# Eight steps instead of four in one tile of the bias product, and another order of the loads at the start

## The chip, the cores and the metric

The kernel runs on one core of a Trainium2 chip. The metric is the device time of one execution in microseconds (us). Five engines work side by side, each through its own list of instructions in order: TensorE (PE, matrix products), VectorE (DVE), ScalarE (ACT), GpSimd (POOL) and SyncE (SP). SP, ACT and POOL also issue DMAs, which 16 DMA engines carry out. An instruction that waits holds up all that stand behind it on its engine.

## What is computed

Four layers are computed one after the other on an image of 2 x 512 x 32 x 32. The change lies in the first, an attention with sampled keys. Cut to what matters:

```python
q    = gconv1x1(bn(x), qw)                     # 8 groups of 64 channels
off  = tanh(pw(gelu(dwconv(q)))) * 4           # where to sample: 8 x 8 points per image and group
kv   = grid_sample(bn(x), off)
k, v = gconv1x1(kv, kw), gconv1x1(kv, vw)
pos  = grid_q[:, :, None, :] - grid_kv[:, None, :, :]      # 1024 queries x 64 points, 2 numbers
bias = sign(pos) * log1p(abs(pos))
bias = relu(bias @ cpb_w1 + cpb_b1)            # 2 -> 128
bias = relu(bias @ cpb_w2 + cpb_b2)            # 128 -> 128
bias = bias @ cpb_w3 + cpb_b3                  # 128 -> 1
attn = softmax(q @ k.T * scale + bias)
x    = x + out_w @ (attn @ v) + out_b
...                                            # an MLP, then three more attention layers
```

The small network from 2 numbers to 1 runs for each of 16 (image, group) x 1024 x 64 pairs, and most of the first layer's time goes there.

## The kernel before

`layer0` holds the first layer. It begins with a top: loads, small products that prepare weights, and the folds of a later layer's weights (`fold`, `small_fold`, `transposed`). Then comes the long loop, `for i in range(steps)`, of 8 x 32 steps: 8 tile pairs t (two groups of one image), 32 steps for each, four points in each step.

A step has four parts, in the order 1, 0, 3, 2 (turns k = 0 to 3). For each, `second` (matmul at L621) multiplies the four points' first hidden layer, tiles `h1`, by 32 columns of `cpb_w2` into a PSUM tile z, and ScalarE (L630) writes its ReLU into a tile `h2`. `first` (L604, VectorE) makes `h1` some steps ahead in a ring of six tiles. `joined` (L635, VectorE) adds part 1 to part 0 and part 3 to part 2, with signs sorted beforehand so that a sum will do for the last weights. A DMA that accumulates, issued by GpSimd (L939, the join), adds the second sum to the first, in `joins[i]`.

`joins[i]` has 128 rows, 32 for each of four points, and all rows of one point are only to be summed with signs. So further DMAs fold it: L932 adds odd rows to even rows (64 rows are left), and four steps share one tile `whole`. The first step of four is folded once more in place (L934, 32 rows); of the others SP copies 32 rows into the tile (L936) and GpSimd adds the other 32 (L942). Then `third` (L650) multiplies four such tiles by `w3_16` into the PSUM tile sim, 16 steps in a call, two calls for each tile pair; `scores` (L658) adds q times k. GpSimd issues in a step the fold of step i-2 (turn 0), the join of i-1 (turn 1), the accumulation of i-3 (turn 1) and, in every fourth step, the second fold (turn 3). Each waits for the semaphore of the DMA whose data it reads. The last 16 steps (from `LAST`) share a tile by two.

`h2` of part 0, where the joins live, comes from two cycles, `h2j` (two slices of the tile `bridge` and two tiles of their own) and `h2p` (six slices of `bridge`); that of part 2, which the join reads, from the pool `h2b` with three tiles. z, and many small PSUM tiles, share a pool of three (`ps_z`, helper `zt`).

Other work of the layer is put between the parts, one piece after every second part, by `behind`, a chain of generators: `finish(t)` (softmax, projection at L710), `offsets(t + 2)` and `samples(t + 1)`. The order on each engine is that of the program text; no planner moves it.

In the top, SP loads the small weights: `load_groups("qw")` and `("kw")` fill the diagonal blocks of tiles that GpSimd has set to zero before, and they are the third to sixth DMA of SP. ScalarE loads x's first quarter and the fold weights. Query weights scaled by the normalisation (`qws`) are kept for all four pairs, and value weights (`vwbd`) too.

Of the kernel before, what the change touches and what calls it, by code (L numbers as in the profile page):

```python
# [19 lines left out]
P = 128  # L20
# [59 lines left out]
def kernel(ctx: ExitStack, tc: tile.TileContext, a: dict, out: bass.AP):  # L80
# [111 lines left out]
    def layer0(l0, fold_d, t2_b, o2_b):  # L192
# [7 lines left out]
        h2p = cycle([bridge[:, k, :] for k in range(6)])  # L200
        h2j = cycle([bridge[:, 6, :], bridge[:, 7, :], *(one.tile([P, HW], F32, name=f"h2j{k}") for k in range(2))])
# [16 lines left out]
        nc.scalar.dma_start(out=xs[0][:, 0, :], in_=a["x"][0, 0:P, :])  # L218
        qkv2, proj2 = load_w(wa, "wa", [a["qkv2_w"], a["proj2_w"]], nc.scalar)
        qkw = next(h2j).rearrange("p (j q n) -> p j q n", j=2, q=NPAIR)  # L220
        vw = one.tile([P, NPAIR, P], F32, name="vwbd")
        bd = {"qw": qkw[:, 0], "kw": qkw[:, 1], "vw": vw}
        for w in bd.values():
            nc.gpsimd.memset(w, 0.0)

        def load_groups(name):
            for h in range(2):
                r = slice(h * DH, (h + 1) * DH)
                nc.sync.dma_start(out=bd[name][r, :, r], in_=a[name][:, r, :].rearrange("q p o -> p q o"))

        load_groups("qw")
        load_groups("kw")
# [4 lines left out]
        ring += [qkv2.rearrange("p k n -> p (k n)")[:, k * 2 * HW : (k + 1) * 2 * HW] for k in range(3)]  # L237
        ring.append(proj2.rearrange("p k n -> p (k n)"))
        vb2 = one.tile([P, CC], F32, name="vb2")
        with nc.allow_non_contiguous_dma("512 numbers"):  # L240
            nc.sync.dma_start(out=vb2, in_=a["vb"][1].rearrange("(k p) -> p k", p=P))
        nc.sync.dma_start(out=xs[0][:, 1:, :], in_=a["x"][0, P:, :].rearrange("(k p) n -> p k n", p=P))

        def late_loads():
            load_groups("vw")
            nc.sync.dma_start(out=xs[1], in_=a["x"][1].rearrange("(k p) n -> p k n", p=P))
# [7 lines left out]
        qws = one.tile([P, NPAIR, P], F32, name="qws")  # L254
        nc.vector.tensor_scalar(qws[:, 0, :], bd["qw"][:, 0, :], s1[:, 0:1], None, ALU.mult)
        qb = one.tile([P, NPAIR], F32, name="qb")
        pqb = zt([P, NPAIR], "pqb")
        for pr in range(NPAIR):
            nc.tensor.matmul(pqb[:, pr : pr + 1], bd["qw"][:, pr, :], col("bn1_b", pr), start=True, stop=True)
        nc.vector.tensor_copy(qb, pqb)  # L260
# [16 lines left out]
        w3_16 = one.tile([P, 48], F32, name="w3_16")  # L277
# [7 lines left out]
        def bias_weights():  # L285
# [5 lines left out]
            few = one.tile([P, 28], F32, name="few")  # L291
# [69 lines left out]
            quarter = few[:, 26:28]  # L361
            for k in range(2):
                nc.vector.tensor_reduce(quarter[:, k : k + 1], ident[:, 2 + k : P : 4], AX.X, ALU.add)
                nc.vector.scalar_tensor_tensor(eighth, quarter[:, k : k + 1], 8.0, eighth, ALU.mult, ALU.add)
            nc.vector.tensor_scalar(w3_16[:, 16:32], row[:, 0:16], eighth, 0.0, ALU.add, ALU.is_equal)
            nc.vector.tensor_scalar(w3_16[:, 16:32], w3_16[:, 16:32], w3sign[:, 1:2], None, ALU.mult)
# [15 lines left out]
        def offsets(t):  # L382
# [4 lines left out]
            for half in range(2):  # L387
                n = slice(half * HALF, (half + 1) * HALF)
                nc.tensor.matmul(pq[:, n], qws[:, pr, :], xs[b][:, pr, n], start=True, stop=True)
# [60 lines left out]
            pos = two.tile([P, 2, 32], F32, name="pos")  # L450
# [14 lines left out]
            sgn = two.tile([P, 2, 32], F32, name="sgn")  # L465
# [19 lines left out]
        def samples(t):  # L485
# [5 lines left out]

            gp = gps.pop(t)
# [7 lines left out]
            near = two.tile([P, 2, 32], F32, name="near")  # L500
            wsum = two.tile([P, 3], F32, name="wsum")
            for ax in range(2):
                nc.scalar.activation(near[:, ax, :], ir, AF.Abs, bias=gp[:, ax : ax + 1], scale=-1.0)
                nc.scalar.activation(
                    near[:, ax, :], near[:, ax, :], AF.Relu, bias=1.0, scale=-1.0, accum_out=wsum[:, ax : ax + 1]
                )
            nc.vector.tensor_mul(wsum[:, 2:3], wsum[:, 0:1], wsum[:, 1:2])
# [33 lines left out]
            nc.tensor.matmul(pkv[:, 1, :], bd["vw"][:, pr, :], kv, start=True, stop=True)  # L541
# [17 lines left out]
        NCH = NR // 4  # L559
        LAST = NT * NR - 16  # L560
        tabs_of = {}

        def load_tabs(c):
# [4 lines left out]
            for ax in range(2):  # L568
                src = slog_d[t, ax].rearrange("(q r) i -> q r i", q=4)
                tab = (one if ax else two).tile([P, 16, 32], F32, name=f"tab{ax}")  # L570
                if 4 * c < LAST:
                    q, r = rc % 4, rc // 4 * 16
# [41 lines left out]
        def second(i, h1s, part):  # L614
# [13 lines left out]
            ring = h2q if part % 2 else h2b if part else h2j if i % (4 if i < LAST else 2) else h2p  # L628
            h2 = ring.tile([P, HW], F32, name="h2", tag="h2") if ring in (h2q, h2b) else next(ring)
# [10 lines left out]
        def third(sim, r, h2s, fours=(), halves=range(2), wide=False):  # L640

            for half in halves:
                n = slice(half * HALF, (half + 1) * HALF)
                w = w3_16[:, 16 - r : 48 - r] if wide else w3[:, 24 - r : 56 - r]
# [17 lines left out]
        def finish(t, sim):  # L662

            b, pr = divmod(t, NPAIR)
            if pr == 0:
                aTs[b] = one.tile([P, NPAIR, HW], F32, name="aT")
            simb = one.tile([P, HW], F32, name="simb", tag="wy")
# [22 lines left out]
            nc.vector.tensor_tensor(atv, atv, sm.unsqueeze(2).to_broadcast([P, 16, NJ]), ALU.mult)  # L690
            yield
# [85 lines left out]
        def transposed(j, k):  # L777
# [4 lines left out]
            for i in range(2):  # L782
                nc.scalar.copy(nat[j][i][:, :, k * P : (k + 1) * P], tw[:, 2 * i : 2 * i + 2, :])
# [4 lines left out]
        def key_weights():  # L788
# [15 lines left out]

        steps = offsets(0)
        advance(steps, 2)
        bias_steps = bias_weights()
        next(bias_steps)
        key_steps = key_weights()
        advance(key_steps)  # L810
        advance(steps, 4)
        advance(bias_steps)
        advance(steps, 20)
        drain(key_steps)
        nc.vector.tensor_tensor(
            qws[:, 1:], bd["qw"][:, 1:], s1[:, 1:].unsqueeze(2).to_broadcast([P, NPAIR - 1, P]), ALU.mult
        )
# [3 lines left out]
        nat = [[next(h2p).rearrange("p (k n) -> p k n", k=2) for _ in range(2)] for _ in range(3)]  # L821
        wq, wk, wv = [lambda o, n, w=w: w[o // 2][:, o % 2, n] for w in nat]
        everything = slice(0, C)
        pb2 = ps_s.tile([P, CC], F32, name="pb2", tag="sim")
# [19 lines left out]
        def small_fold():  # L844

            row = zt([P, C], "row")
            for o in range(CC):
                nc.tensor.matmul(
                    row[:, o * P : (o + 1) * P], col("qkv2_b", o).to_broadcast([P, P]), ident, start=True, stop=True
                )  # L850
            yield
# [4 lines left out]
            for m in range(CC):  # L856
                n = slice(m * P, (m + 1) * P)
                accumulate(pb2[:, m : m + 1], [(proj2[:, o, n], vb2[:, o : o + 1]) for o in range(CC)])
                yield
            nc.vector.tensor_tensor(o2_b, pb2, col("proj2_b", 0, CC), ALU.add)  # L860

        fold_steps, small_steps = fold(), small_fold()
        for k in range(CC):
            for j in range(3):
                transposed(j, k)

        advance(fold_steps)
        drain(bias_steps)
        advance(steps)
        advance(fold_steps)  # L870
        drain(steps)
        advance(small_steps)
        advance(fold_steps)
        advance(small_steps)
# [3 lines left out]
        for _ in range(5):  # L878
            advance(fold_steps)
            advance(small_steps)  # L880
        drain(fold_steps)

        steps = NT * NR
        h1s, parts, joins, sim, w1s = {}, {}, {}, None, None  # L890
        behind = chain(small_steps, offsets(1), samples(0))
# [5 lines left out]
        for i in range(steps):  # L897
            for k, part in enumerate((1, 0, 3, 2)):
# [5 lines left out]
                due = i - 20  # L904
                if k == 1 and 0 <= due < LAST and due % 16 == 0:
                    t, r = divmod(due, NR)
                    if r == 0:
                        sim = ps_s.tile([P, HW], F32, name="sim")
                    third(sim, r, [joins.pop(due + j) for j in range(0, 16, 4)], wide=True)
                    if r:  # L910
# [10 lines left out]
                if LAST <= i - 2 and i < steps - 2:  # L921
# [4 lines left out]
                    if i - 3 >= LAST and i % 2 and k == 3:  # L926
                        nc.gpsimd.dma_start(out=joins[i - 3][1:P:2], in_=joins.pop(i - 2)[1:P:2], accum_op=ALU.add)
                if 0 <= i - 2 < LAST:
                    j = (i - 2) % 4
                    whole, own = joins[i - 2 - j], joins[i - 2]  # L930
                    if k == 0:
                        nc.gpsimd.dma_start(out=own[0:P:2], in_=own[1:P:2], accum_op=ALU.add)  # L932
                    if k == 3 and j == 0:
                        nc.gpsimd.dma_start(out=own[0:P:4], in_=own[2:P:4], accum_op=ALU.add)  # L934
                    if k == 3 and j:
                        nc.sync.dma_start(out=whole[j:P:4], in_=own[0:P:4])  # L936
# [3 lines left out]
                j = (i - 3) % 4  # L940
                if k == 1 and 0 <= i - 3 < LAST and j:
                    nc.gpsimd.dma_start(  # L942
                        out=joins[i - 3 - j][j:P:4], in_=joins.pop(i - 3)[2:P:4], accum_op=ALU.add
                    )
# [5 lines left out]
                if k == 1 and due == LAST:  # L950
                    third(sim, 16, [joins.pop(due + j) for j in range(0, 8, 2)])
# [1325 lines left out]
```

## Time and profile before

| | |
|---|---|
| time, median of 3 runs | 3342.97 us (3342.06 to 3345.39) |
| the profiled execution: its time, its span | 3343.91 us, 3342.0 us |
| matmuls of L621 (z) | 16384, 593 ns each; four run side by side |
| chain that ended last: TensorE's share, L621's share | 96%, 52% |
| the loop | from 57.4 to about 1968 us |
| DMA engines' busy share, 400 to 1000 us | 0.79 |
| software queue (GpSimd's DMAs), whole span | 68400 packets, 231.26 MB |

A line of the page reads: line of the code, engine, operation, output<-input, count, busy time and mean length, then how long the engine stood idle just before such instructions and what ended that. In a timeline a line begins with start and length. The length of a DMA instruction is that of its issue; when its data has landed is seen from what waits for it.

### The profile page before, as it was taken

Reading aid. Unit: us, or ns where it says so; the run is one execution under the profiler, and the core shown is the slowest. Engines: PE = TensorE matmul, PEld = TensorE weight load, DVE = VectorE, ACT = ScalarE, POOL = GpSimd, SP = SyncE. Lnnn points to the kernel's source line nnn. Section 1 sums busy time; section 2 is a strip of 40 time slices with the busy share of each in tenths; the row PEclk is TensorE's granted clock in tenths of the full one; section 3 lists DMA queues with packets and bytes.
Section 4 is the critical chain, followed back from the end, with each engine's and each line's share of the span. In section 5 each row is a group of like instructions: output and inputs, shape, how many; then the busy total and the mean of one; then the engine's idle time right before and its main releaser. Section 6 shows DMA issues by size and latency. Waiting matters only on the chain.

```text
span 3342.0 us, 60958 instructions
## 1 busy us (share of the span) xinstructions
PE 3319.8 (99%) x24813; PEld 1605.2 (48%) x24813; DVE 2640.9 (79%) x3029; ACT 1809.4 (54%) x2774; POOL 675.3 (20%) x803
## 2 busy tenths in 40 slices
PE   9999999999999999999999999999999999999999
PEld 4333333333333333333333339999953443687777
DVE  6999999999998799999999966455446465765556
ACT  4866877877876677877867642112126245122221
POOL 1333333333333233333333210000000000000000
PEclk9999999999999999999999999999999999999999
DMA  5777877787787577778877741000100000000111
GB/s 171 158 162 161 162 164 156 158 169 152 160 166 158 107 165 151 161 165 160 166 159 152 161 120 58 14 9 12 51 0 14 26 32 17 7 7 4 29 33 36
DMA packets 142482, 343.91 MB, mean 103 GB/s; under 512 B 36465, under 2 KB 51441, under 8 KB 141425
## 3 DMA queue, kind: packets, MB, share of 16 engines
q0 software_dynamic: 68400, 231.26, 37.1%
q1 hardware_dynamic: 72496, 103.95, 10.1%
q8 instruction: 197, 3.23, 0.4%
q10 hardware_dynamic: 1296, 4.72, 0.4%
q14 instruction: 93, 0.75, 0.1%
HBM read 71.46 MB, written 10.83 MB: 25 GB/s over the span
## 4 chain that ended last, share of the span: by engine, by line
PE 96%; DVE 1%; issue 1%; ACT 1%; DMA 1%; SPq 0%; POOL 0%; DVEq 0%; ACTq 0%; POOLq 0%
PE z L621 52%; PE pma L135 6%; PE pw L1440 6%; PE pmb L135 5%; PE pmv L1440 4%; PE score L1619 3%; PE pv L1631 3%; PE pm L1440 3%; PE score L1440 3%; PE ppr L1440 1%; PE pmt L1440 1%; PE sim L650 1%; PE pf L135 1%; PE pp L710 1%; PE pma L1343 1%
## 5 line engine op out<-in xcount | busy, mean ns | idle before, releaser
L621 PE MATMUL z<-wa,cpb_w 128*32 128x512 f32 x10880 | 1191.9, 593 | 2.7 <-ACT h L630 2.7
L630 ACT ACTIVATE h<-z,b2h 128x1024 f32<-128x1024 f32 x768 | 851.1, 1113 | 331.0 <-PE z L621 301.7
L604 DVE CUSTOM_DVE_ANT_1 wa<-tab,pairs 128x2048 f32<-128x2048 f32 x340 | 776.4, 2284 | 3.1 <-PE z L621 2.6
L621 PEld LDWEIGHTS z<-wa,cpb_w 128*32 128x32 f32 x10880 | 346.5, 110 | 809.3 <-issue 712.4
L621 PE MATMUL z<-h,cpb_w 128*32 128x512 f32 x5504 | 609.5, 593 | 0.7 <-ACT h L630 0.7
L604 DVE CUSTOM_DVE_ANT_1 h<-tab,pairs 128x2048 f32<-128x2048 f32 x172 | 392.7, 2284 | 1.7 <-PE z L621 1.5
L621 PEld LDWEIGHTS z<-h,cpb_w 128*32 128x32 f32 x5504 | 175.1, 110 | 407.9 <-issue 362.7
L635 DVE SCALAR_TENSOR_TENSOR h<-h,turn,h 128x1024 f32<-128x1024 f32 x256 | 327.1, 1278 | 5.5 <-ACT h L630 5.5
L630 ACT ACTIVATE bridge<-z,b2h 128x1024 f32<-128x1024 f32 x162 | 180.8, 1116 | 119.0 <-PE z L621 119.0
L932 POOL DMA_DIRECT2D bridge<-bridge x150 | 127.5, 850 | 539.5 <-DMA bridge<-h 517.5
L635 DVE SCALAR_TENSOR_TENSOR bridge<-bridge,turn,h 128x1024 f32<-128x1024 f32 x162 | 207.0, 1278 | 4.3 <-ACT bridge L630 4.3
L939 POOL DMA_DIRECT2D bridge<-h x161 | 158.4, 984 | 247.0 <-DVE h L635 151.8
L1283 ACT COPY p<-pma 128x128 f32<-128x128 f32 x80 | 21.3, 266 | 334.7 <-PE pma L135 334.7
L1275 DVE TENSOR_TENSOR upper<-pma,p 128x256 f32<-128x256 f32 x80 | 33.7, 421 | 178.6 <-ACT p L1283 178.5
L1620 ACT ACTIVATE p<-score 128x512 f32<-128x512 f32 x256 | 130.0, 624 | 81.2 <-PE score L1619 79.4
L932 POOL DMA_DIRECT2D h2j<-h2j x90 | 76.2, 846 | 314.7 <-DMA h2j<-h 292.6
L630 ACT ACTIVATE h2j<-z,b2h 128x1024 f32<-128x1024 f32 x94 | 104.9, 1116 | 41.5 <-PE z L621 41.5
L1652 DVE TENSOR_TENSOR acc<-acc,p 128x1024 f32<-128x1024 f32 x96 | 111.0, 1217 | 19.5 <-ACT p L1620 19.2
L1619 PE MATMUL score<-q,k 64*128 64x512 f32 x512 | 120.7, 604 | 1.1 <-DVE gm L1196 1.1
L635 DVE SCALAR_TENSOR_TENSOR h2j<-h2j,turn,h 128x1024 f32<-128x1024 f32 x94 | 120.1, 1278 | 0.0
L1631 PE MATMUL pv<-p,vT 128*64 128x512 f32 x512 | 116.5, 598 | 0.0
L942 POOL DMA_DIRECT2D bridge<-bridge x90 | 111.1, 1235 | 0.2 <-issue 0.2
(460 smaller groups left out, 4379.4 us busy)
## 6 DMA issues: line engine op xcount, KB each, us to landing
bridge<-h POOLq DMA_DIRECT2D x161, 512.0 KB, 5.5
h2j<-h POOLq DMA_DIRECT2D x94, 512.0 KB, 5.5
bridge<-bridge POOLq DMA_DIRECT2D x159, 256.0 KB, 3.7
tab<-slog_d SPq DMA_DIRECT2D x128, 256.0 KB, 5.0
h2j<-h2j POOLq DMA_DIRECT2D x90, 256.0 KB, 3.3
bridge<-bridge POOLq DMA_DIRECT2D x150, 128.0 KB, 5.4
bridge<-bridge SPq DMA_DIRECT2D x90, 128.0 KB, 3.6
bridge<-h2j SPq DMA_DIRECT2D x90, 128.0 KB, 3.7
```

What stands on the lines that cost most here:

```text
L135: nc.tensor.matmul(pm, w, m, start=(k == 0), stop=(k == len(pairs) - 1))
L604: nc.vector._custom_dve(TENSOR_ADD_SAT, out=h1, in0=tx.unsqueeze(1).to_broadcast([P, H, 2, W]), in1=ty.unsqueeze(3).to_broadcast([P, H, 2, ...
L621: nc.tensor.matmul(z[point * 32 : point * 32 + 32, n], cpb_w2[:, lo : lo + 32], h1s[point][:, half * 16 : half * 16 + 16, :], start=True, ...
L630: nc.scalar.activation(h2, z, AF.Relu, bias=b2h[:, part : part + 1])
L635: nc.vector.scalar_tensor_tensor(h2, h2, turn[:, part // 2 : part // 2 + 1], parts.pop(part + 1), ALU.mult, ALU.add)
L932: nc.gpsimd.dma_start(out=own[0:P:2], in_=own[1:P:2], accum_op=ALU.add)
L939: nc.gpsimd.dma_start(out=joins[i - 1], in_=other, accum_op=ALU.add)
L942: nc.gpsimd.dma_start(out=joins[i - 3 - j][j:P:4], in_=joins.pop(i - 3)[2:P:4], accum_op=ALU.add)
L1440: nc.tensor.matmul(out, stationary(l, k), moving(r, k), start=start and k == 0, stop=k == nk - 1, skip_group_check=not start,)
L1619: nc.tensor.matmul(sc, ks[m][r, s * P : (s + 1) * P], qs[m][r, n], start=True, stop=True)
L1620: nc.scalar.activation(p[:, part], sc, AF.Exp, scale=64 ** -0.5)
L1631: nc.tensor.matmul(pv[half][part * 64 : part * 64 + 64], vt[s % 4][:, lo : lo + 64], lps[s, half][:, part, :], start=(s == 0), stop=(s == 7),)
```

## The change

It has two parts. In the loop, eight steps instead of four share one tile for the first seven tile pairs. The second fold is now made for each of those steps, and a third fold, from 32 rows to 16, for the first of eight; of the seven others SP copies 16 rows and GpSimd adds 16. `third` takes four tiles of eight steps with the new weights `w3_32`, in one call for each tile pair, one step later than the second call came before. The last pair's first half stays with four steps in a tile. On GpSimd the join of step i-1 is issued ahead of the first fold of step i-2, the second fold has moved to the next step's beginning, and the accumulation stands after the first fold. The tiles come from one queue `room` of 11, to which a tile returns when it has been read (`taken`). In `samples` the near weights are split over two pieces of `behind`.

At the top, the query weights are ScalarE's first DMAs; the tiles' off-diagonal blocks alone are set to zero; the fold weights are loaded in larger DMAs, the key weights and the rest of x later and by ScalarE too; a part of the transposes comes earlier, the key transposes later; a transpose of four blocks is copied by one instruction; the small bias product is made with rows of 512; `qws` and `vws` hold one pair and are loaded anew for each.

```diff
-        h2p = cycle([bridge[:, k, :] for k in range(6)])
-        h2j = cycle([bridge[:, 6, :], bridge[:, 7, :], *(one.tile([P, HW], F32, name=f"h2j{k}") for k in range(2))])
+        room = deque([bridge[:, 7, :], *(one.tile([P, HW], F32, name=f"h2j{k}") for k in range(3))])
+        room += [bridge[:, k, :] for k in range(7)]
...
-        for w in bd.values():
-            nc.gpsimd.memset(w, 0.0)
+        for h in range(2):
+            r, other = [slice(k * DH, (k + 1) * DH) for k in (h, 1 - h)]
+            for w in bd.values():
+                nc.gpsimd.memset(w[r, :, other], 0.0)
...
         load_groups("qw")
-        load_groups("kw")
+        nc.scalar.dma_start(out=xs[0][:, 0, :], in_=a["x"][0, 0:P, :])
+        load_rows(qkv2, "qkv2_w", 0, 1)
+        load_rows(qkv2, "qkv2_w", 1, 2)
+        load_rows(qkv2, "qkv2_w", 2, 4)
...
+        def load_group(w, name, pr):
+            for h in range(2):
+                r = slice(h * DH, (h + 1) * DH)
+                nc.sync.dma_start(out=w[r, r], in_=a[name][pr, r, :])
...
+                if ax == 0:
+                    yield
...
+        WIDE = (NT - 1) * NR
         LAST = NT * NR - 16
+
+        def shared(i):
+            return 8 if i < WIDE else 4 if i < LAST else 2
...
-            for i in range(2):
-                nc.scalar.copy(nat[j][i][:, :, k * P : (k + 1) * P], tw[:, 2 * i : 2 * i + 2, :])
+            nc.scalar.copy(nat[j][:, :, k * P : (k + 1) * P], tw)
...
+        load_rows(proj2, "proj2_w", 0, 4)
+        for j in range(3):
+            transposed(j, 0)
+        load_groups("kw")
...
+            nc.scalar.dma_start(out=vb2, in_=a["vb"][1].rearrange("(k p) -> p k", p=P))
+
+        nc.scalar.dma_start(out=xs[0][:, 1:, :], in_=a["x"][0, P:, :].rearrange("(k p) n -> p k n", p=P))
...
-            for m in range(CC):
-                n = slice(m * P, (m + 1) * P)
-                accumulate(pb2[:, m : m + 1], [(proj2[:, o, n], vb2[:, o : o + 1]) for o in range(CC)])
                 yield
-            nc.vector.tensor_tensor(o2_b, pb2, col("proj2_b", 0, CC), ALU.add)
+            pb = zt([P, C], "pb")
+            for k in range(CC):
+                nc.tensor.matmul(
+                    pb[32 * k : 32 * k + 32],
+                    vb2[:, k : k + 1].to_broadcast([P, 32]),
+                    proj2[:, k, :].rearrange("p (m q) -> p q m", m=CC),
+                    start=True,
+                    stop=True,
+                )
...
-                due = i - 20
-                if k == 1 and 0 <= due < LAST and due % 16 == 0:
...
-                    third(sim, r, [joins.pop(due + j) for j in range(0, 16, 4)], wide=True)
-                    if r:
+                for due, n, turn_of in ((i - 37, 8, 3), (i - 20, 4, 1)):
+                    if k != turn_of or not 0 <= due < LAST or due % NR or shared(due) != n:
+                        continue
+                    t = due // NR
+                    sim = ps_s.tile([P, HW], F32, name="sim")
+                    third(sim, 0, [taken(due + j) for j in range(0, 4 * n, n)], wide=w3_32 if n == 8 else w3_16)
+                    if n == 8:
...
-                if 0 <= i - 2 < LAST:
-                    j = (i - 2) % 4
-                    whole, own = joins[i - 2 - j], joins[i - 2]
-                    if k == 0:
-                        nc.gpsimd.dma_start(out=own[0:P:2], in_=own[1:P:2], accum_op=ALU.add)
-                    if k == 3 and j == 0:
+                for at in (i - 3, i - 4):
+                    if not 0 <= at < LAST:
+                        continue
+                    n = shared(at)
+                    j, late = at % n, i - 4 - at
+                    own, whole = joins.get(at), joins.get(at - j)
+                    if (k, late) == (0, -1) and (n == 8 or j == 0):
                         nc.gpsimd.dma_start(out=own[0:P:4], in_=own[2:P:4], accum_op=ALU.add)
-                    if k == 3 and j:
-                        nc.sync.dma_start(out=whole[j:P:4], in_=own[0:P:4])
+                    elif (k, late) == (0, 0) and n == 8 and j == 0:
+                        nc.gpsimd.dma_start(out=own[0:P:8], in_=own[4:P:8], accum_op=ALU.add)
+                    if j and (k, late) == ((3, -1) if n == 8 else (0, -1)):
+                        nc.sync.dma_start(out=whole[j:P:n], in_=own[0:P:n])
+                    elif j and (k, late) == ((2, 0) if n == 8 else (3, -1)):
+                        nc.gpsimd.dma_start(out=whole[j:P:n], in_=own[n // 2 : P : n], accum_op=ALU.add)
+                        taken(at)
                 if k == 1 and i - 1 in parts:
                     other = joined(parts.pop(i - 1), 2)
                     nc.gpsimd.dma_start(out=joins[i - 1], in_=other, accum_op=ALU.add)
-                j = (i - 3) % 4
-                if k == 1 and 0 <= i - 3 < LAST and j:
-                    nc.gpsimd.dma_start(
-                        out=joins[i - 3 - j][j:P:4], in_=joins.pop(i - 3)[2:P:4], accum_op=ALU.add
-                    )
+                if k == 1 and 0 <= i - 2 < LAST:
+                    own = joins[i - 2]
+                    nc.gpsimd.dma_start(out=own[0:P:2], in_=own[1:P:2], accum_op=ALU.add)
```

## The prediction

> **What bounds the kernel now.** I read the page first: busy time by engine, the chain of waits by line, the costliest groups; then the busy time in a stretch of the long loop, the chain in order of time, and the timelines of TensorE and GpSimd there.
>
> ```profile
> PE 3319.8 (99%) x24813; PEld 1605.2 (48%) x24813; DVE 2640.9 (79%) x3029; ACT 1809.4 (54%) x2774; POOL 675.3 (20%) x803
> 400.00:1000.00 600.00, 597.99 (x5432) 186.78 (x5428) 580.73 (x380) 455.10 (x623) 210.32 (x245) 1.00 0.79 160
> ...
> 792.94 5.29 PE z L621 x48
> ...
> 1025.43 1.90 PE L650 MATMUL sim<-bridge,w 128*32 128x512 f32 x16
> 1027.26 1.98 PE L658 MATMUL sim<-x,kqs 128*128 128x512 f32 x4
> ...
> 1029.25 5.29 PE z L621 x48
> L932 POOL DMA_DIRECT2D bridge<-bridge x150 | 127.5, 850 | 539.5 <-DMA bridge<-h 517.5
> ```
>
> TensorE is the bound: 597.99 of 600 us busy in the loop, and its busy time falls only if matmuls are taken out. One period of the loop (one tile pair, 32 steps) is 1029.25 - 792.94 = 236.3 us, 7.38 us a step. The third product, L650, starts 1.83 us ahead of the next group at 1025.43, and 1.72 us at 1883.93 and 1935.43. VectorE has 3% idle. GpSimd is busy little, but it mostly stands waiting for a DMA: that is the row to watch, because its wait is not idleness that another instruction of its queue could use.
>
> ```profile
> 320.13 0.84 POOL L932 DMA_DIRECT2D h2j<-h2j  x1 [4.67 <-DMA h2j<-h]
> 320.66 1.22 POOL L939 DMA_DIRECT2D h2j<-h  x1
> 321.23 1.51 POOL L942 DMA_DIRECT2D bridge<-bridge  x1
> 326.51 0.86 POOL L932 DMA_DIRECT2D h2j<-h2j  x1 [3.77 <-DMA h2j<-h]
> ...
> 523.32 0.85 POOL L932 DMA_DIRECT2D h2j<-h2j  x1 [2.53 <-DMA h2j<-h]
> 523.86 1.22 POOL L939 DMA_DIRECT2D h2j<-h  x1
> 529.62 0.83 POOL L932 DMA_DIRECT2D h2j<-h2j  x1 [4.55 <-DMA h2j<-h]
> 530.15 1.22 POOL L939 DMA_DIRECT2D bridge<-h  x1
> ```
>
> Each line is a start and a length. L932 is the first fold (256 KB), L939 the join (512 KB), L942 the last accumulation (128 KB). The reader is to see two things. When GpSimd is behind, its cycle is a latency: fold, join 0.53 later, next fold when that join has landed, 529.62 - 523.32 = 6.30 us. And three DMAs issued in a row end at 320.97, 321.88 and 322.74: about 0.86 us each to make, one after the other. Over the whole timeline 83 cycles have the join within 0.6 us of the fold; 48 of them take 6.26 to 6.34, and the mean is 6.69, since table loads and other transfers lengthen some to 7 to 9 us. So GpSimd can go round in 6.69 where the period gives it 7.38: it keeps pace by 0.7 us a step.
>
> **What the Trainium skill says.** "DMA: Bandwidth & Descriptors", section "SWDGE vs HWDGE vs iDMA": accumulating in a DMA can only be issued from GpSimd, whose cores compute the descriptors in software, for the one queue there is. The trace agrees: the folds' 68400 packets are all in one software queue, and the 0.86 us each is that work. The same page, "Anatomy of one DMA — SWDGE (gpsimd) path": about 2 us of a DMA is fixed, most of it the receipt of the last byte. Here 256 KB landed in 3.3 us and 512 KB in 4.85 when alone (medians of the loop and of unqueued joins), so 0.36 us for each of the 4 packets more per DMA engine, and 1.9 us fixed: the fixed part agrees, the rate is lower than the page's. "Two DMAs through the same engine are not ordered": a dependent DMA must wait for the first one's semaphore on the issuing engine; that is the wait in brackets above.
>
> **The change, part by part.**
>
> *Third product.* Before, each period has two calls of L650, 16 recorded matmuls each; after, with eight steps' sums laid into one tile, one call. In the last period nothing goes (its first half is folded fourfold as before, the rest by two). So 7 calls x 1.72 = 12.0 us less on TensorE, which is the bound: -12.0. The period becomes 234.6, 7.33 a step.
>
> *Top.* The first use of the query weights waits: pqb starts 8.92, 1.52 after the warm-up matmuls end at 7.40. They are loaded by SP after 0.99 us of memsets and take 6.6 us to land. After, they are ScalarE's first DMAs, free of the memsets (which now leave the loaded blocks alone), ahead of x and the fold weights: -1.5. The small bias product pb is four times 0.79 on the chain (16 matmuls of one column); it becomes four of 512 columns on four column groups, 8 recorded matmuls at the 0.107 that L621's make in a row (13.73/128): 0.9, so -2.3. Key transposes, row and three quarters of pqb only change place: 0. ScalarE's 24 copies of 0.24 become 12 of some 0.53, and two key loads, vb and the rest of x (0.7, 0.7, 0.43, 0.38 of issue) now stand before its copy of prow, behind which are the pw2t product and the transposes on TensorE: bounded between +2 (all of it exposed) and -2 (the 0.59s of the key copies leave the path); I take 0. Sum of the top -3.8. What is late next is TensorE's own row of folds (28 us of pf), which nothing in the change shortens.
>
> *VectorE and ScalarE in the loop.* A query scaling per period (0.29, the L255 row's length) and a few more small reductions at the top. VectorE is busy 228.7 of 236.3 and waits 2.9 for ScalarE (1.8 simbias, 1.1 kvbd): 231.9 against 234.6, so hidden, by 2.7 us. The near weights are split over two slots: TensorE's one wait for ScalarE per period, 0.67, should go. But the scores come three slots later, so twelve of the exponentials' slots (0.87 a slot) now fall beside a table scaling (0.70 and 0.73) while one of three z buffers is held: a gap of 1.6 where the wait of 0.67 came from 1.9. Ends -4.7 and +5 over seven periods; taken as 0. Per-pair weight loads (64 KB at a time or less) and their SP issues have most of a period to land: 0.
>
> *GpSimd's queue.* This decides. After, per step: second fold of step i-3 (128 KB), join of i-1 (512), first fold of i-2 (256), accumulation of i-4 (64). The second fold waits for the first fold issued two places ahead in the same queue; the first fold now lies behind a join in the DMA queue; and the next join is queued behind the waiting second fold. Three DMAs instead of two are in each turn of the latency. Cycle: before, 0.86 to make the fold + 12 packets x 0.36 (4 + 8) + 1.0 receipt + 0.1 = 6.3, as measured. After: 0.86 + 0.86 to make second fold and join, join and first fold 12 x 0.36 (the second fold's 2 packets pass while the join is made), 1.0 + 0.1: 7.15. Every eighth step has a third fold (64 KB) in the same place, one more 0.86: +0.11 a step. The lengthening by other transfers was 6.69 - 6.29 = 0.40; SP's copies fall from 24 rows a step (32 x 3/4) to 14 (16 x 7/8) and the tables stay, so 0.30. Together 7.56, against 7.33 that TensorE gives: 0.23 too long, over 7 x 32 = 224 steps 51 us. Not all is paid: the tile of eight is read 2.25 steps (16.5 us) after its last accumulation's turn, which lands in 5.6, so about 10 us of lag is free, once at the start and once again after the four pp products in mid-loop (4 x 7.06 without steps let the queue catch up). 51 - 20 = +31. Who waits: TensorE at the third product, and ScalarE for the join's source buffer (three of them), then TensorE behind it. Bounds: with excess 0.22 and the third fold nearly free (one packet each, 0.36 / 8: 7.15 + 0.05 + 0.22 = 7.42): 0.09 x 224 = 20, within the slack, so 0; with excess 0.40: 7.66, 74 us, none caught up.
>
> *Tail.* The last sixteen steps fold as before, half a step later, with 1.5 steps in hand: 0.
>
> Sum: -12.0 - 3.8 + 31 = +15. The profiled execution took 3343.91 (span 3342.0); the median 3342.97 lies 0.9 below it. 3342.97 + 15 = 3358.
>
> **Rivals.**
> 1. *The queue keeps pace* (ends on the other side). If the cycle averages 7.35 or less, only the savings show: 3342.97 - 15.8 = 3327. For it: the first fold's packets may overlap the join's, and 7.15 alone is below 7.33. It turns at an excess plus third fold of 0.18 a step. Against: the 0.40 is measured.
> 2. *The queue takes about what TensorE gives*: cycle 7.47, 0.14 x 224 = 31, less 20, and the top smaller by 2: about 3341.
> 3. *The queue is worse*: 7.66 and no catching up, 74 - 15.8: 3401. For it: the stretch from 508 to 552 already averages 7.4 a cycle.
> 4. *VectorE becomes the bound*: needs 2.7 us more a period than counted; nothing adds that. If it did by 1 us, 7 us: 3334. Within rival 1's share.
>
> **How the numbers follow.** My forecast 0.47, rival 1 (with 4) 0.28, rival 2 0.15, rival 3 0.10. This kernel's runs lie within 0.1%; 0.2%, 6.7 us, is what can be told from no change. Slower: 0.47 + 0.10 = 0.57; same 0.15; faster 0.28. The forecast's own range is 3350 to 3385; the range must take in rival 1 down to 3325 and part of rival 3: 3325 to 3392.
>
> **What would show it.** Right: L650's calls halved in the loop; GpSimd's second fold waiting each step for a first fold that lands some 6 us after issue; start-to-start of joins above 7.4 for long stretches with no wait for VectorE; TensorE idle before the third product, released by a DMA, and ScalarE waiting for the join. The first z matmul near 53.6 instead of 57.4. Wrong: TensorE still 99.6% busy in the loop with joins waiting for VectorE (rival 1), or a first z later than before. The whole forecast falls if first folds land in under 5.5 us behind a join.

## The result and the profile after

The changed kernel takes 3530.01 us (median of 6 runs, 3528.12 to 3536.93) against 3343.55 (6 runs, 3342.06 to 3346.13): a ratio of 1.0559 [1.0547, 1.057], 186.5 us more. The profiled execution's span is 3530.2 us.

Four lines of the page after, to be held against those of before: busy time by engine, shares of the chain by engine, one group of GpSimd's, and one kind of DMA with its size and its median time from issue to landing. The fifth is the same kind of DMA on the page before.

```profile
PE 3368.6 (95%) x24677; PEld 1592.7 (45%) x24677; DVE 2652.4 (75%) x3049; ACT 1801.7 (51%) x2763; POOL 861.3 (24%) x1030
...
PE 50%; DMA 31%; issue 9%; POOL 8%; DVE 2%; ACT 1%; SPq 0%; POOLq 0%; DVEq 0%; ACTq 0%
...
L1000 POOL DMA_DIRECT2D bridge<-bridge x157 | 131.4, 837 | 736.2 <-DMA bridge<-bridge 704.7
...
bridge<-bridge POOLq DMA_DIRECT2D x172, 256.0 KB, 6.6
...
bridge<-bridge POOLq DMA_DIRECT2D x159, 256.0 KB, 3.7
```

The chain of waits was 96% TensorE; now it is half TensorE, 31% DMA and 8% GpSimd. L1000 is the second fold. It waits for a DMA about 4.5 us each time (704.7 us by 157 instructions in this tile alone), and what it waits for is the first fold (256 KB). Over all 240 first folds the median from issue to landing is 6.65 us, where it was 3.3 before.

Busy time in the same stretch of the loop, 400 to 1000 us, in the page's order of engines, then granted clock and DMA share:

```profile
400.00:1000.00 600.00, 556.47 (x4865) 165.21 (x4867) 526.24 (x345) 415.43 (x584) 250.51 (x295) 0.97 0.78 146
```

TensorE is busy 556.47 of 600 us where it was busy 597.99, VectorE 526.24 where it had 580.73, and the DMA engines' share is 0.78 where it was 0.79: nobody is full. This is the picture of a latency. GpSimd's timeline shows it (start, length, line; in brackets the idle time before and what ended it):

```profile
521.58 0.84 POOL L1000 DMA_DIRECT2D h2j<-h2j  x1 [4.37 <-DMA h2j<-h2j]
522.12 1.19 POOL L1010 DMA_DIRECT2D h2j<-h  x1
522.66 1.52 POOL L1013 DMA_DIRECT2D h2j<-h2j  x1
523.20 1.78 POOL L1006 DMA_DIRECT2D bridge<-bridge  x1
530.02 0.84 POOL L1000 DMA_DIRECT2D h2j<-h2j  x1 [5.04 <-DMA h2j<-h2j]
530.56 1.19 POOL L1010 DMA_DIRECT2D bridge<-h  x1
```

L1000 is the second fold, L1010 the join, L1013 the first fold, L1006 the accumulation of 16 rows. Four instructions are issued in a row, then comes a wait for the third of them. The next join (530.56) has no wait of its own: it stands behind L1000, and the sum that it reads was ready some 8 us before. In what follows a turn is one round of this queue, from one second fold to the next (not one of the four turns k of a step). This one is 530.02 - 521.58 = 8.44 us. The chain in order of time is the same story without a gap:

```profile
521.58 0.84 POOL h2j L1000
522.41 0.07 POOL h2j L1010
522.48 0.17 issue
522.66 7.09 DMA h2j<-h2j
529.74 0.28 issue
530.02 0.84 POOL h2j L1000
530.86 0.07 POOL bridge L1010
530.92 0.17 issue
531.10 6.31 DMA h2j<-h2j
```

In 217 of the 224 turns of the first seven tile pairs the join did not wait. Without a third fold (189 of them) the shortest is 7.34 and the mean 8.20; with one (28) the mean is 8.52; together 8.24. TensorE would give 7.33. If the other seven turns lost as much, that is 0.91 x 224 = 204 us. The loop, from the first z matmul to the next layer's first (L135, pma), took from 57.36 to 2010.46 before and takes from 53.90 to 2198.12 after, 191.1 us more, though matmuls have left it. The kernel of experiment 1 below has the same matmuls, and against its loop (54.20 to 2000.99) it is 197.4 us more.

How the lag reaches TensorE is in its waits (whole span; us in total, times, longest):

```profile
ACT h L665 <- DMA bridge<-h: 158.6, 61, 4.5
...
PE z L656 <- ACT h L665: 64.1, 65, 3.2
```

ScalarE writes its ReLU into a buffer that an earlier join still reads (158.6 us, and 49.7 more for joins into the tiles h2j), and TensorE waits for z behind it. TensorE also waited for `ow` (L581, 23.4 us, 6 times) and for `qpad` (12.2): these are no part of the folds. `ow` is a load in SP's queue behind a copy that waits for a late second fold, and `qpad` is set to zero by GpSimd, behind the waiting folds.

At the top the first z matmul is at 53.90 instead of 57.36.

```profile
7.10 0.28 PE L275 MATMUL pqb<-pc,bridge 128*128 128x1 f32 x2
...
44.49 2.41 PE L906 MATMUL pb<-wa,vb 128*32 128x512 f32 x8
...
53.90 7.07 PE L656 MATMUL z<-h,cpb_w 128*32 128x512 f32 x64
```

### The profile page after: what moved, and what is told of

Its sections match the earlier page's. It is cut to its first block, busy times and chain, and to the rows that moved or that the text cites. A ratio compares the mean times of both kernels' runs of the same rounds, so it can differ in the third digit from the quotient of the medians.

```text
span 3530.2 us, 61204 instructions
## 1 busy us (share of the span) xinstructions
PE 3368.6 (95%) x24677; PEld 1592.7 (45%) x24677; DVE 2652.4 (75%) x3049; ACT 1801.7 (51%) x2763; POOL 861.3 (24%) x1030
## 3 DMA queue, kind: packets, MB, share of 16 engines
q10 hardware_dynamic: 3248, 6.56, 0.5%
## 4 chain that ended last, share of the span: by engine, by line
PE 50%; DMA 31%; issue 9%; POOL 8%; DVE 2%; ACT 1%; SPq 0%; POOLq 0%; DVEq 0%; ACTq 0%
DMA bridge<-bridge 20%; DMA h2j<-h2j 10%; PE z L656 9%; PE pma L135 6%; PE pw L1509 5%; PE pmb L135 5%; PE pmv L1509 4%; PE score L1688 3%; PE pv L1700 3%; POOL bridge L1000 3%; PE pm L1509 3%; PE score L1509 3%; PE pp L749 1%; POOL h2j L1000 1%; PE ppr L1509 1%
## 5 line engine op out<-in xcount | busy, mean ns | idle before, releaser
L656 PE MATMUL z<-wa,cpb_w 128*32 128x512 f32 x10880 | 1218.0, 599 | 58.4 <-ACT h L665 48.6
L656 PE MATMUL z<-h,cpb_w 128*32 128x512 f32 x5504 | 618.0, 596 | 18.7 <-ACT h L665 15.5
L1000 POOL DMA_DIRECT2D bridge<-bridge x157 | 131.4, 837 | 736.2 <-DMA bridge<-bridge 704.7
L1013 POOL DMA_DIRECT2D bridge<-bridge x164 | 250.9, 1530 | 3.4 <-issue 2.0
L1010 POOL DMA_DIRECT2D bridge<-h x175 | 207.1, 1184 | 120.6 <-DVE h L670 107.8
L670 DVE SCALAR_TENSOR_TENSOR bridge<-bridge,turn,h 128x1024 f32<-128x1024 f32 x176 | 226.1, 1285 | 8.6 <-ACT bridge L665 8.5
L665 ACT ACTIVATE bridge<-z,b2h 128x1024 f32<-128x1024 f32 x176 | 196.2, 1114 | 66.8 <-PE z L656 56.4
L1006 POOL DMA_DIRECT2D bridge<-bridge x106 | 177.1, 1671 | 24.7 <-DMA bridge<-bridge 24.3
L1000 POOL DMA_DIRECT2D h2j<-h2j x71 | 59.3, 836 | 349.6 <-DMA h2j<-h2j 337.0
L1013 POOL DMA_DIRECT2D h2j<-h2j x76 | 114.4, 1505 | 0.9 <-DMA h2j<-h 0.9
```

Of the source, the lines that this page charges most:

```text
L656: nc.tensor.matmul(z[point * 32 : point * 32 + 32, n], cpb_w2[:, lo : lo + 32], h1s[point][:, half * 16 : half * 16 + 16, :], start=True, ...
L665: nc.scalar.activation(h2, z, AF.Relu, bias=b2h[:, part : part + 1])
L670: nc.vector.scalar_tensor_tensor(h2, h2, turn[:, part // 2 : part // 2 + 1], parts.pop(part + 1), ALU.mult, ALU.add)
L1006: nc.gpsimd.dma_start(out=whole[j:P:n], in_=own[n // 2 : P : n], accum_op=ALU.add)
L1010: nc.gpsimd.dma_start(out=joins[i - 1], in_=other, accum_op=ALU.add)
```

## The experiments

All are compared with the kernel before, a median of 3343.42 us beside them (3343.85 beside the runs of experiment 6). "The changed kernel" is 3530.

**1. The same DMAs in another order.** The second and third fold are issued behind the join:

```diff
-                    if (k, late) == (0, -1) and (n == 8 or j == 0):
-                        nc.gpsimd.dma_start(out=own[0:P:4], in_=own[2:P:4], accum_op=ALU.add)
-                    elif (k, late) == (0, 0) and n == 8 and j == 0:
-                        nc.gpsimd.dma_start(out=own[0:P:8], in_=own[4:P:8], accum_op=ALU.add)
...
                     nc.gpsimd.dma_start(out=joins[i - 1], in_=other, accum_op=ALU.add)
+                for at in (i - 3, i - 4):
+                    if k != 1 or not 0 <= at < LAST:
+                        continue
+                    n, own = shared(at), joins.get(at)
+                    if at == i - 3 and (n == 8 or at % n == 0):
+                        nc.gpsimd.dma_start(out=own[0:P:4], in_=own[2:P:4], accum_op=ALU.add)
+                    elif at == i - 4 and n == 8 and at % n == 0:
+                        nc.gpsimd.dma_start(out=own[0:P:8], in_=own[4:P:8], accum_op=ALU.add)
```

> The changed kernel with the second and third fold issued behind the join of the same step instead of ahead of it; nothing else moves. Theory Q (a chain of latencies in GpSimd's queue: the next join stands behind a second fold that waits for a first fold which itself lies behind a join): the join no longer waits for a landing, only the DMA engines' own work is left, 15 packets x 0.36 = 5.4 us a step and some 0.75 of other transfers, under the 7.33 TensorE gives: 3325 to 3335 us. Rival T (the added DMA work itself, whatever its order): the same DMAs run, so above 3480. Rival S (the cost sits in the top, in SP's queue or in ScalarE's bunched work): unchanged, about 3530.

3334.64 us (3333.85 to 3338.2), 0.9976 [0.9966, 0.9985]: 195 us below the changed kernel with the same bytes, the same number of DMAs and the same matmuls. Theory Q (the order in GpSimd's queue makes a latency chain) holds, the two others fall. GpSimd's timeline in this kernel; L1006 is the join here, L1012 the second fold, L1017 the first fold, L1002 the accumulation:

```profile
509.72 0.91 POOL L1006 DMA_DIRECT2D bridge<-h  x1 [2.89 <-DVE h L670]
510.28 1.21 POOL L1012 DMA_DIRECT2D bridge<-bridge  x1
510.80 1.57 POOL L1017 DMA_DIRECT2D bridge<-bridge  x1
511.36 1.82 POOL L1002 DMA_DIRECT2D h2j<-bridge  x1
516.51 0.90 POOL L1006 DMA_DIRECT2D h2j<-h  x1 [3.33 <-DVE h L670]
```

A line of its waits in the same stretch as above, 400 to 1000 us, and its busy times there:

```profile
POOL bridge L1006 <- DVE h L670: 137.9, 39, 5.8
```

```profile
400.00:1000.00 600.00, 598.20 (x5424) 186.38 (x5420) 586.25 (x386) 460.62 (x630) 281.82 (x330) 1.00 0.86 165
```

GpSimd waits for VectorE's sum, in other words for work that paces the loop, and TensorE is busy 598.20 of 600 again. The second fold now stands one place behind the join and asks for a first fold issued a step before, which has mostly landed: the second folds wait 40.4 us in all in these 600 us.

**2. The top alone**, with the folds of before:

> The changed kernel's top (and its pool of tiles, per-pair weight loads and split near weights) with the folds, their order and the two third products of the kernel before. Q and T: only the top's gain shows, the first z matmul at 53.9 instead of 57.4, so 3338 to 3341 us. S: the loss stays, above 3400.

3337.39 us (3336.45 to 3340.09), 0.9983 [0.9975, 0.999], a little better than expected: the whole loss comes with the loop's new folds. This kernel also has the near weights split over two slots (a slot is one place in a step where `behind` puts a piece of other work), which experiment 7 takes apart.

**3 to 5. What is in the turn: the sixteen rows.** The changed kernel without the accumulations, without SP's copies, and without both; what these kernels leave out is missing from their sums. The edit for both:

```diff
-                        nc.sync.dma_start(out=whole[j:P:n], in_=own[0:P:n])
+                        if n != 8:
+                            nc.sync.dma_start(out=whole[j:P:n], in_=own[0:P:n])
...
-                        nc.gpsimd.dma_start(out=whole[j:P:n], in_=own[n // 2 : P : n], accum_op=ALU.add)
+                        if n != 8:
+                            nc.gpsimd.dma_start(out=whole[j:P:n], in_=own[n // 2 : P : n], accum_op=ALU.add)
```

> The changed kernel without the accumulations of 16 rows into the shared tile in the first seven tile pairs (the sums of seven steps in eight are then only half there). The prediction's cycle was 7.15 at best and 7.56 on the mean, measured 7.34 and 8.24. If the accumulation issued right behind the first fold delays that fold's landing, the cycle falls by 0.4 or more and the time to 3400 to 3440; if it does not lie in the chain, the time stays at 3510 to 3530.

> The changed kernel without SP's copies of 16 rows into the shared tile in the first seven tile pairs (the accumulations then add to stale rows). The copy becomes due when the second fold has landed, which is while the join and the first fold are under way. If its packets get between those of the chain, the cycle falls by 0.3 to 0.5 and the time to 3410 to 3460; if not, 3510 to 3530.

> The changed kernel without both the copies and the accumulations of 16 rows into the shared tile in the first seven tile pairs (seven steps in eight are left out of the sums there). Alone, each took 0.24 us off the mean cycle of 8.20 (7.96 both times), and 56 and 33 us off the time. If they disturb the chain in two different places, the cycle falls to 7.7 and the time to 3430 to 3450, and what is left above 7.15 is that of the other transfers; if in the same place, cycle 7.9 and 3465 or more.

**6. What else: the tables.** Loaded once for all steps, in the changed kernel, in the one before, and in the changed one together with both edits above:

```diff
-                tab = (one if ax else two).tile([P, 16, 32], F32, name=f"tab{ax}")
...
-                    nc.sync.dma_start(out=tab, in_=src[q, r : r + 16, :].partition_broadcast(P))
...
-                tabs_of[c].append(tab)
+            if not raw:
+                src = slog_d[0, 0].rearrange("(q r) i -> q r i", q=4)
+                raw.append(one.tile([P, 16, 32], F32, name="raw"))
+                nc.sync.dma_start(out=raw[0], in_=src[0, 0:16, :].partition_broadcast(P))
+            tabs_of[c] = [raw[0], raw[0]]
```

> The changed kernel with the position tables loaded once and used for every stretch of steps, instead of two loads of 256 KB for every four steps: its output is of other positions. Same instructions on every engine but SP. Asked: what lengthens GpSimd's cycle from its floor of 7.34 to a mean of 8.24. Theory X (the table loads, which pass the fold's and the join's packets in the DMA engines, are a large share): mean 7.85 or less, so 0.4 x 224 = 90 us or more off 3530: 3445 or less. Theory Y (the copies, the accumulations and the folds themselves make it): mean 8.1 or more, 3500 to 3530.

> The same edit in the kernel before: tables loaded once. There the cycles in which GpSimd is behind (the join within 0.6 us of the fold) average 6.69 against 6.29 for the floor. X: the 0.40 is the tables', the mean falls to 6.45 or less. Y: it stays at 6.6 or more. The time stays within 5 us of 3343 by both, since GpSimd keeps pace.

> The changed kernel without the accumulations and copies of 16 rows, and with the tables loaded once. If tables, copies and accumulations are all that lengthens the cycle, it stands near its floor of 6.92 nearly always and below the 7.33 that TensorE gives: 3325 to 3350. If more than these (other loads, the folds' own queueing), the cycle stays above 7.4 in the mean and the time is above 3370.

GpSimd's turns in the changed kernel and its variants (second fold to second fold, join not waiting), and the times, one run each except the first:

| left out | shortest | mean, no third fold | mean with third fold | time |
|---|---|---|---|---|
| nothing | 7.34 | 8.20 | 8.52 | 3530.01 |
| accumulations | 6.92 | 7.96 | 8.61 | 3474.02 |
| copies | 7.28 | 7.96 | 8.81 | 3496.83 |
| both | 6.92 | 7.71 | 8.70 | 3429.82 |
| tables | 7.35 | 8.07 | 8.49 | 3500.44 |
| all three | 6.92 | 7.39 | 8.18 | 3358.83 |

The accumulation costs 0.42 in the shortest turn and 0.24 in the mean. The copy costs next to nothing in the shortest (0.06) and 0.24 in the mean. Both together cost 0.42 and 0.49: the means add, as was expected if they act in two places (7.7 was named). Of this 0.49 the shortest turn already has 0.42. The mean stands 0.86 above the shortest turn with nothing left out and still 0.79 without both, so most of the lengthening above the floor is not the sixteen rows'. Each alone saved 56 and 33 us, which lies between the two ranges that were named for it; both saved 100, which is 3429.82 at the edge of the range.

The tables alone come to 0.13, or 30 us: theory Y for the changed kernel. Once the sixteen rows are gone, the tables are worth 71 us and 0.32 of the mean, so the shares don't add; why was not tried.

In the kernel before, with the tables once, the mean goes from 6.69 (83 turns) to 6.64 (39 turns), in 3343.31 us: theory Y by its number. But these are not the same turns. Those with a second fold, which fall in the steps in which the next tables are loaded, go from 7.73 (12 turns) to 6.73 (8); those with fold, join and accumulation alone from 6.56 (37) to 6.81 (18). So what lengthened the turns there is not settled by this run.

Without all three, 67 of 184 turns are below 7.0, as in this stretch of GpSimd's timeline (6.97):

```profile
518.38 0.83 POOL L990 DMA_DIRECT2D bridge<-bridge  x1 [4.41 <-DMA bridge<-bridge]
518.92 1.19 POOL L1002 DMA_DIRECT2D bridge<-h  x1
519.46 1.52 POOL L1005 DMA_DIRECT2D bridge<-bridge  x1
525.35 0.83 POOL L990 DMA_DIRECT2D bridge<-bridge  x1 [4.37 <-DMA bridge<-bridge]
```

Here L990 is the second fold. Even so the kernel takes 3358.83, between the two ranges expected and above the kernel before: the other order with all of these DMAs takes 3334.64. What makes up the last 0.47 between 6.92 and 7.39 was not tried. Other transfers of the program alone it cannot be: of 105 turns longer than 7.05 in this trace, 89 have no DMA beside them but the joins and folds.

**7. The parts that gain, and a better version.** On the other order and on the top alone, the split of the near weights is taken back; then the softmax's exponentials go two to a slot instead of three:

```diff
-                if ax == 0:
-                    yield
...
-                if g % 3 == 2:
+                if g % 2 == 1:
                     yield
```

> The kernel with the join first, and the near weights of the samples in one piece again. In that kernel the exponentials and the samples' weights stand 1.5 steps later against the table scalings than before. Theory B (ScalarE's bunched work holds one of three z buffers): the near weights no longer lie beside a table scaling in any case, and splitting them only moves the next pieces into one: 3330 to 3334 us, against 3334.6. Rival (the split is a gain wherever it stands, as it seemed with the top alone): 3336 to 3339.

> The top alone, without the split of the near weights. The first z matmul stands 3.5 us earlier in the kernel with the top, but its time is 6.0 us below the kernel before. If the split took away ScalarE's one wait per period (0.67, seven times at most), this kernel lies between: 3339.5 to 3341 us. If the whole 6 us come from the top: 3337.4 as with the split.

> The kernel with the join first, near weights in one piece, and the sixteen exponentials spread over eight slots of two instead of six of three. Theory B: with the table scaling beside them the gap on ScalarE falls from 1.6 to 1.3 us, and TensorE's waits there (0.42 and 0.2 a period) go: 2 to 4 us below the kernel with the near weights whole. Rival: the period's lost 0.9 us lies elsewhere: the same within 1 us, or slower because the later pieces now fall beside table scalings.

| kernel | time (range) | ratio to before |
|---|---|---|
| other order | 3334.64 (3333.85 to 3338.2) | 0.9976 [0.9966, 0.9985] |
| other order, near weights whole | 3333.08 (3331.74 to 3333.6) | 0.9969 [0.9957, 0.9982] |
| the same, exponentials by two | 3331.49 (3328.83 to 3333.47) | 0.9963 [0.995, 0.9977] |
| top alone | 3337.39 (3336.45 to 3340.09) | 0.9983 [0.9975, 0.999] |
| top alone, near weights whole | 3340.13 (3338.68 to 3342.1) | 0.9989 [0.9983, 0.9996] |

The top is worth 3.3 us. By the medians the split is worth 2.7 with the old slots of the scores, where TensorE's waits for ScalarE at z (4.0 us, 6 times) are gone with it; with the eight-step tile, whose scores come three slots later, the medians have it 1.6 worse. Exponentials by two save another 1.6 by the medians, less than the 2 to 4 expected. In each of these three pairs the intervals overlap, so none of them is told apart from nothing with certainty. The folds in the other order with near weights whole and exponentials by two are then worth 8.6 (3340.13 - 3331.49), of 12.0 that left TensorE. That version is the fastest run here: 0.37% below the kernel before, and 5.6% below the changed one.

## Why the prediction was right or wrong

*What bounds, and the direction: right.* Slower was the likeliest case, with GpSimd's turn as the cause: "the second fold waits for the first fold issued two places ahead in the same queue" and "the next join is queued behind the waiting second fold". Experiment 1 shows that the loss comes from this order: the same transfers in the other order lose nothing. The signs named for it are there: calls of the third product (now L685) about halved in the loop (15 to 8), the second fold waiting each step for a fold that landed in 6.65 us, joins seldom waiting for VectorE (in 7 of 224 turns they waited for anything of their own), ScalarE waiting for the join's source, and TensorE idle before third products until a DMA landed (15.8, 11.7, 11.2 and 3.1 us by tile).

*The size: wrong, 3358 against 3530, outside the range.* The step that failed is "Together 7.56, against 7.33": the turn was 8.24. Most of the miss lies in one term of that sum, the lengthening by other transfers. By its terms:

- The floor, "7.15", was 7.34. Without the accumulation it is 6.92, so the sum was 0.23 too high for what it counted (its 0.36 for a packet is not the reason: the two medians that it comes from, 4.85 and 3.3 for 4 packets more, give 0.39). And it left out the accumulation, which is issued right behind the first fold and costs 0.42. Together +0.19. The kernel before had given no sign of this cost: there 128 KB are accumulated right behind the awaited join, and the turns with it (37, shortest 6.26, median 6.32) are as short as those without (34, 6.29 and 6.31).
- The lengthening, "0.30", was 0.86: +0.56, the mis-sized term. I had taken the 0.40 of the kernel before and made it smaller, since the copies fall from 24 rows a step to 14. Bytes were the wrong measure (128 KB of tables a step were worth 0.13 of the mean, the sixteen rows' 112 KB 0.49), and so were these turns: before, only 83 of 239 were on the latency, those in which GpSimd was behind; now nearly every one is. What fills the 0.86 is known in part. Without the sixteen rows 0.79 is left above the shortest turn, without the tables too 0.47, and that remainder is open.
- The third fold, "+0.11", was (8.52 - 8.20) / 8 = 0.04: -0.07.
- "about 10 us of lag is free, once at the start and once again": the loop lost 197 us where the turns give 204, so at most some 7 of the 20 were seen. That other parts of the loop feel the lag before the third product does, ScalarE at the join's source above all, fits the waits shown; it was not tried by itself.

The first three make 0.68 x 224 = 152 us, the fourth some 13 (20 less 7), of the 172 between 3358 and 3530; 2 to 3 more are the third product's, below, and a few us are not assigned. The upper bound, 74, was built from an excess of 0.40; the largest that I took was the one measured where GpSimd was not the bound.

*Who waits: incomplete.* The join's source buffer was named and is the largest wait. Not named were SP, whose copies wait for the late second folds with the tables and `ow` behind them, and `qpad`, zeroed in GpSimd's own queue.

*Third product, -12.0: right in kind, too large.* 16 recorded matmuls a period have gone. Of the 12 us, 8.6 show in the time when the queue keeps pace. The rest is not waiting: between the top alone with the near weights whole and the fastest version TensorE's busy time in the loop falls by 9.5 us (1945.25 to 1935.73), and its idle time there is the same (8.1 and 8.2). So the 1.72 for a call was too high a price; the exponentials beside the table scalings (+5 as its end, 0 taken) do not show in these totals.

*Top, -3.8: right in sum, 3.3 by time, with some luck.* The first z was forecast at 53.6 and stands at 53.90. Query weights: pqb at 7.10 instead of 8.92, so -1.8 where -1.5 was taken. The bias product takes 2.41, not 0.9: its 8 matmuls overlap, but each lasts 1.05 to 1.44 us where one of z's has 0.59, so the 0.107 taken from z was no price for them. Their rows are read in a rearranged order (`p q m`) and z's are not; that this is the reason was not tried. Before it was 4 x 0.79 on the chain, so -0.8 and not -2.3. The first z comes 3.46 earlier, so what was taken as 0 brought about 0.9 more: this and the query weights' 0.3 made up for most of the bias product's 1.5.

*VectorE: hidden, as said* (526.24 of 600; in the other order 586.25).

*Rivals.* Rival 1, the queue keeps pace, is what the other order does: 3334.64, and 3331.49 at best, against 3327. Rival 3 had the right sign of the miss and was still 129 us short. Rivals 2 and 4 did not come: the turn was longer than TensorE's, and VectorE had time to spare.

## What to carry to other kernels

In a queue that is worked in order, look at every instruction that waits and count how many places back its producer stands. Here, with the producer two places back, its full latency became a part of every turn, and everything queued behind it paid. Move the oldest step's work behind the newest step's independent work, so that the producer has a step's time to land; here that is worth 195 us with not one byte less. When a latency chain just fits on paper, price its lengthening from turns in which it always binds, with every small transfer that becomes due inside the turn, and not from the bytes; where no such turns exist, say that the lengthening is not known.

## What was not expected of the hardware

- In the changed kernel a DMA of 64 KB is not cheap: leaving out the accumulation shortens the shortest turn by 0.42 us, from 7.34 to 6.92, though it is issued after the DMA that ends the turn. It is not so wherever an accumulation stands behind an awaited DMA: in the kernel before, 128 KB behind the join cost nothing (6.26 against 6.29 at the shortest). What makes the difference was not tried. The Trainium skill's "DMA: Bandwidth & Descriptors", section "SWDGE vs HWDGE vs iDMA", has the descriptors made in software by GpSimd's cores. The instruction lengths fit work that is queued there, 0.84, 1.19, 1.52, 1.78 for issues 0.54 apart. But that this, and not the packets, delays the first fold is not shown.
- What is saved by leaving transfers out does not add: the tables are worth 30 us, the sixteen rows 100, all three 171.
- In the changed kernel TensorE is not only idle more often, the same matmuls also keep it busy longer. The whole loop, in the changed kernel and in that of experiment 1 (stretch, its length, then busy time by engine, granted clock and DMA share as above):

```profile
53.90:2198.12 2144.22, 1997.43 (x17123) 602.03 (x17123) 1846.86 (x1227) 1416.98 (x1945) 839.08 (x983) 0.97 0.76 145
54.20:2000.99 1946.79, 1936.73 (x17124) 606.54 (x17123) 1840.34 (x1227) 1426.24 (x1945) 840.24 (x983) 1.00 0.82 160
```

Of the 197.4 us more, 136.7 are TensorE's idle time and 60.7 its busy time, and the granted clock is 0.97 against 1.00. Over whole runs it was 0.984 at 3530 us, 0.994 at 3430 and 0.999 at 3335. That the gaps bring the clock down was not tried by itself. The 60.7 us are not a second cause of the loss: GpSimd's turns, which wait for DMAs and not for TensorE, account for the loop by themselves.
